# An attention and expert kernel: keys and queries of a head loaded in single transfers, the base of the experts' output formed on TensorE, and a planner that knows when the attention output is divided

## The chip, the cores and the metric

The kernel runs on one core of a Trainium2 chip. A core has five engines that run their own instruction streams and meet through semaphores: TensorE (PE in the profile), VectorE (DVE), ScalarE (ACT), GpSimd (POOL) and SyncE (SP), which here does nothing but issue DMAs. The metric is the device time of one execution in microseconds (us); the number for a kernel is the median of its runs. A profile is one further execution, with the hardware profiler on; its span goes from its first to its last instruction.

## The reference, cut to what matters

Two batches (B = 2) of N = 2048 tokens with D = 256 features go through one transformer layer. `mod` is six vectors per batch, made from `c`.

```python
h = layernorm(x) * (1 + ca) + sa
q, k, v = h @ Wq, h @ Wk, h @ Wv                 # 16 heads of 16
R = |i - j|;  R_hat = (1 + exp(v_h)) / (1 + exp(v_h - w_h * R))
scores = relu(q k^T) * R_hat ; causal ; softmax(scores / sqrt(16))
x = x + ga * (ctx @ Wo + bo)
h2 = layernorm(x) * (1 + cb) + sb                # xf: all 4096 tokens
s = softmax(h2 @ gate_w.T)                       # 8 experts
for each expert: take the 512 tokens with the largest s   (top_k)
    y = layernorm(h2[idx]) * ln_w + ln_b
    o = gelu(y @ fc1.T + b1) @ fc2.T + b2 ;  o *= s[idx]
    xf[idx] += o                                 # xf starts as h2
x = x + gb * xf
```

The last line means that a token's output is `x + gb*h2` plus `gb` times what experts add to it. The kernel writes `x + gb*h2` to the output first (this is what the experts' output is added to, here called the base), and then adds the experts' rows with an indirect accumulating DMA.

## The kernel before, in words

**Attention.** The work is cut into units (batch, head, query tiles): for a head, query tiles of 128 are packed as [0-3], [4,5], [6,7], and then 8 to 15 one by one, 11 units a head and 352 in all. A unit's steps are: scores `sc` on PE (L907; keys `kr` times queries `qr`, with 16 rows of contraction), DVE multiplies relu(sc) by the table `tb` (L920) and takes the maximum off (L927), POOL masks the diagonal (L932), PE transposes (L971), ACT takes the exponential (L979), PE multiplies with values `vg` (L1012). When a head is complete, DVE divides by the row sums into `ctx` (L1079, function `divide`).

PE keeps four row groups of 32 rows, so that the 16 rows of a head's keys are needed four times, at partitions 0, 32, 64 and 96. Keys and queries of all heads are first written to DRAM (`k_d`, `q_d`: tiles of 128 x 512, one for 8 heads and 512 tokens) and read back for each head. Before, each read is 16 rows of 512 numbers (32 KB): `keys` issues one for each of four chunks and four row groups, 16 a head; `queries` issues four for each group of four query tiles, 16 a head.

The order of issue on SP for a head h: around the head's first scores the next head's inputs are asked by `head_inputs` (the table `tb`, 1 MB, and the keys; values every fourth head), and the scores of query tile 4c ask for the query group two ahead. There are three buffers for query groups, and two each for keys and tables. SP works its list in order; an issue that has to wait for its buffer holds up all behind it.

**Planner.** The order of PE, DVE, ACT and POOL is written out by a planner in the program (`manual_schedule`): it keeps a clock for each engine (`plan.pe`, `plan.dve`, ...), and at each point chooses the next step of the attention or a "filler": a piece of a prologue (layernorm, q, k, v of the next 512 tokens) or of an epilogue (what follows attention for a group g of 512 tokens). The pieces of an epilogue name the pieces that they wait for; `made` has the planned time of each finished piece. The names used below: `turn` (PE transposes ctx, `trc`, L660, ACT copies it to cT), `project` (PE multiplies by Wo), `add` (adds x1), `stats`/`apply` (layernorm), `rows` (ACT writes z, the tokens as the experts want them, and a DMA of 128 KB takes them to `z_d`; two buffers), `gated` (h2 times gb) and `base` (adds x1, DMA to the output). `over()` is true when the last unit's scores have been issued. `late(i)` says whether fillers lag behind their pace. The last two heads (from unit PAIR_AT) are interleaved by query group.

**Search, listing, experts.** After attention the scores of all tokens lie in 128 x 256 numbers `rows`. A search over the bits of a float finds each expert's threshold, two bits a step in 15 steps: three DVE comparisons with a count (`ge`, L1511), one PE matmul that sums the counts over partitions (`pcnt`, L1516), and a few small DVE operations that set the next candidates. Between the matmul and its use, one piece of the remaining DVE list (`left["dve"]`, the last layernorm statistics) is put in, and ACT writes z rows that are ready. Then come `tot` and `p_off` (L1556, L1558), the listing of chosen tokens, and the gathers by POOL (`zt<-z_d`, L1656). Experts e = 0 to 7 each gather 4 x 128 rows, transpose (`trf`, L1671), do the two layers (`ph`, `pof`) and scatter-add.

For the last batch 16 `gated` and 16 `base` pieces are still undone when attention ends. `rest_of_output` issues them on POOL, each 128 x 256 (L625, the line of the helper `sum_or_product`), after the gathers of expert 0, each base with its DMA to the output:

```python
        gathered(0, s)
        rest_of_output()
```

Of the kernel before, what the change touches and what calls it, by code (L numbers as in the profile page):

```python
# [9 lines left out]
FP = mybir.dt.float32  # L10
# [4 lines left out]
ALU = mybir.AluOpType  # L15
# [4 lines left out]
P = 128  # L20
B = 2
N = 2048
# [150 lines left out]
def adaln_block_kernel(  # L173
# [30 lines left out]


    q_d = [[dram.tile([P, 512], FP, name=f"q_d_{b}_{i}") for i in range(HG * 4)] for b in range(B)]
    k_d = [[dram.tile([P, 512], FP, name=f"k_d_{b}_{i}") for i in range(HG * 4)] for b in range(B)]
    v_d = [[dram.tile([512, 8 * VW], FP, name=f"v_d_{b}_{i}") for i in range(HG * 4)] for b in range(B)]


# [41 lines left out]
    def turned(shape: list, name: str):  # L252

        return ps_tr.tile(shape, FP, name=name, tag=f"tr{plan.bank()}")
# [191 lines left out]
    def prologue(b: int, c: int, hT, first: bool):  # L446
# [56 lines left out]
        def qk(g: int, w_sb, dst, tag: str, parts: list):  # L503
            n = len(parts) * P
            pp = turned([P, n], f"p{tag}_{u}_{g}_{parts[0]}")
            for k in range(DC):
                nc.tensor.matmul(
                    pp, lhsT=w_sb[:, k, ts(g, P)], rhs=s["hT"][:, k, ds(parts[0] * P, n)],
                    start=(k == 0), stop=(k == DC - 1),
                )  # L510
            if parts[0] == 0:
                s[tag, g] = ev_p.tile([P, 512], FP, name=f"{tag}_{u}_{g}", tag="qk")
            nc.scalar.copy(s[tag, g][:, ds(parts[0] * P, n)], pp)
            if parts[-1] == 3:
                nc.sync.dma_start(out=dst[b][g * 4 + c], in_=s[tag, g])
            return plan.small(427 * len(parts), 120 + 120 * len(parts), 0)

        def val(g: int, parts: list):
# [42 lines left out]
        return work  # L561


    def keys(b: int, h: int, c: int):
        for r in range(RG):
            nc.sync.dma_start(
                out=inputs[b, h][0][ds(32 * r, HD), ts(c, 512)],
                in_=k_d[b][h // 8 * 4 + c][ts(h % 8, HD), :],
            )

    def values(b: int, h: int, c: int):
        nc.sync.dma_start(
# [3 lines left out]
            ),  # L576
        )

    def head_inputs(b: int, h: int, chunks=range(4)):
        kr = krp.tile([P, N], FP, name=f"kr_{b}_{h}", tag="kr")  # L580

        tb = tabp.tile([P, N], FP, name=f"tb_{b}_{h}", tag="tab")
        row = rhat_d[h, :]
        nc.sync.dma_start(
            out=tb, in_=bass.AP(tensor=row.tensor, offset=row.offset, ap=[[1, P], [1, N]])
        )

        if h % 4 == 0:
            vg = vgp.tile([P, NQ * 4 * VW + HD], FP, name=f"vg_{b}_{h}", tag="vg")
            nc.gpsimd.memset(vg[:, NQ * 4 * VW :], 0.0)  # L590
        else:
            vg = inputs[b, h - 1][2]
        inputs[b, h] = (kr, tb, vg)
        for c in chunks:
            keys(b, h, c)
            if h % 4 == 0:
                values(b, h, c)

    def queries(at: int):

        if at >= len(asked):
            return
        b, h, c = asked[at]
        qr = qrp.tile([P, 512], FP, name=f"qr_{b}_{h}_{c}", tag="qr")
        for r in range(RG):
            nc.sync.dma_start(
                out=qr[ds(32 * r, HD), :], in_=q_d[b][h // 8 * 4 + c][ts(h % 8, HD), :]
            )
        qrs[b, h, c] = qr


    def epilogue(b: int, g: int):
# [52 lines left out]

        def project(k: int):
            po = turned([P, D], f"po_{u}_{k}")
            for f in range(HG):
                nc.tensor.matmul(
                    po, lhsT=s["cT", k][:, f, :], rhs=wo_sb[:, b, f, :],  # L670
                    start=(f == 0), stop=(f == HG - 1),
                )
            if over():
                x1 = s["x1"][:, k, :]
                nc.vector.tensor_tensor(x1, po, x1, ALU.add)
                s["added", k] = True
                return plan.small(853, 0, 350)

            nc.scalar.copy(s["h2"][:, k, :], po)
            return plan.small(853, 380, 0)  # L680

        def add_to(k: int):
            if ("added", k) in s:
                return 0.0
            x1 = s["x1"][:, k, :]
            return sum_or_product(x1, s["h2"][:, k, :], x1, ALU.add)

# [33 lines left out]
            skip("widen", k)  # L721
            return plan.small(0, 0, 430)

        def skip(name: str, k: int):
            work[:] = [p for p in work if p[3] != (first, name, k)]
            made[first, name, k] = 0.0

        def root():
            s["root"] = root_of(*s["vr", 3], f"3_{u}")
# [18 lines left out]
        def move(k: int):  # L748
            h2 = s["h2"][:, k, :]
            if ("centered", k) in s:  # L750
                nc.vector.scalar_tensor_tensor(
                    h2, h2, s["rs2"][:, k : k + 1], sb, ALU.mult, ALU.add
                )
                return plan.small(0, 0, 430)
            return sum_or_product(h2, h2, sb, ALU.add)


        def gated(k: int):
# [59 lines left out]
            work[0][4].extend((first - 4, x, k) for x in ("base", "gate") for k in K)  # L818
        for k in K:
            piece("pe", 218, turn, "turn", k, ("project", k - 2) if k > 1 else ("begin", 0))  # L820
            if g == 3 and k < 2:
                work[-1][4].append((first - 2, "gate", k + 2))
            piece("pe", 853, project, "project", k, "turn", "bias")
# [58 lines left out]
    FIRST_OUT = 11  # L882
    SOON = ("load", "bias", "begin", "turn", "project", "add")
    LOW = ("gated", "base", "rows", "stats3", "power3", "root3", "shift3")
    row_free = [0.0, 0.0]
    OPEN = 4
    groups_out = [[epilogue(b, g) for g in range(4)] for b in range(B)]
# [3 lines left out]
    def over():  # L891
        return begun[0] == len(units)
# [165 lines left out]
    def divide():  # L1058

        b, h, gs = dividing.pop(0)  # L1060
        if gs[-1] == 3:
            undivided.remove((b, h))
        if h == 0:
            ctxs[b] = cxp.tile([P, NQ, D], FP, name=f"ctx_{b}", tag="ctx")
        cs = sums[b, h][0]
        rc = avp.tile([P, NQ], FP, name=f"rc_{b}_{h}_{gs[0]}", tag="rc")
        g0, gn = gs[0], len(gs)
        nc.vector.reciprocal(
            rc[:, 0 : 4 * gn].rearrange("p (q o) -> p q o", o=1),
            cs[:, ds(4 * g0, 4 * gn), HD:VW],  # L1070
        )

        o = ctxs[b][:, ds(4 * g0, 4 * gn), ts(h, HD)].rearrange("p (g j) f -> p g j f", j=4)
        if h % 2:
            o = bass.AP(
                tensor=o.tensor, offset=o.offset + 3 * D,
                ap=[list(o.ap[0]), list(o.ap[1]), [-D, 4], list(o.ap[3])],
            )
        nc.vector.tensor_tensor(  # L1079
            o, cs[:, ds(4 * g0, 4 * gn), 0:HD].rearrange("p (g j) f -> p g j f", j=4),  # L1080
            rc[:, 0 : 4 * gn].rearrange("p (g j o) -> p g j o", j=4, o=1)
            .broadcast_to([P, gn, 4, HD]),
            ALU.mult,
        )
        plan.small(0, 0, 200 + 150 * gn)
        if h == H - 1:
            add(groups_out[b][gs[0]][1], False)
            i = turns[-1]["i"] if turns else 0
            more(max(i, H * len(PACKS)), FIRST_OUT * len(PACKS) if b < B - 1 else 12)
# [40 lines left out]

    def make(w: dict, at: int):
        p = w["work"].pop(at)
        w["past"] = p[2]() or 0.0
        if not w["in_order"]:
            made[p[3]] = w["past"]
        if not w["work"]:
            fillers.remove(w)
# [143 lines left out]

    def late(i: int):

        return ahead_by(i) < (1.5 if plan.now == "f" else -1.5)

    def ahead_by(i: int) -> float:

# [9 lines left out]
    with tc.manual_schedule(engines={ENG.PE, ENG.DVE, ENG.Activation, ENG.Pool}):  # L1297
# [10 lines left out]
            arrived(c)  # L1308

        def arrived(c: int):  # L1310
            keys(0, 0, c)
            queries(c)
            values(0, 0, c)
            there[c] = plan.act + 5000
            if c == 3:
                head_inputs(0, 1)
                after_chunks()
# [76 lines left out]
    def weights(e: int):  # L1394
# [14 lines left out]
            lambda p=p: (p[2](), done.add(p[3])) for p in pending if p[0] == "dve"  # L1409
        ],  # L1410
        "act": [p for p in pending if p[0] == "act"],
        "pool": [p for p in pending if p[0] == "pool"],
    }

    def ready_rows():

# [3 lines left out]
                done.add(p[3])  # L1420
                left["act"].remove(p)

    def rest_of_output():
        for p in left["pool"]:
            assert all(x in done for x in p[4])
            p[2]()
            done.add(p[3])

    with tc.manual_schedule(engines={ENG.PE, ENG.DVE, ENG.Activation, ENG.Pool}):
        b1_sb = rt.tile([P, E * FC], FP, name="b1_sb")  # L1430
# [12 lines left out]
        nc.gpsimd.iota(steps, pattern=[[0, TOP // 2 + 1], [1, 3]], base=1, channel_multiplier=0)  # L1443
        nc.gpsimd.iota(twice, pattern=[[2, TOP // 2 + 1], [0, 3]], base=0, channel_multiplier=0)
        nc.vector.tensor_tensor(steps, steps, twice, ALU.logical_shift_left)
        thr = rt.tile([P, 1], I32, name="thr0", tag="thr", bufs=2)
        nc.vector.memset(thr, 0)

# [58 lines left out]
        for bit in range(TOP, -1, -2):  # L1507
# [9 lines left out]
            if bit:  # L1517
# [2 lines left out]
                    base, steps[:, bit // 2 - 1, :], thr.broadcast_to([P, 3]), ALU.bitwise_or  # L1520
                )

            if left["dve"]:
                left["dve"].pop(0)()
                ready_rows()
# [14 lines left out]

        while left["dve"]:
            left["dve"].pop(0)()
            ready_rows()

        hit = rt.tile([P, 2, 2, P], FP, name="hit")
        for k, op in ((0, ALU.is_gt), (1, ALU.is_equal)):
# [173 lines left out]
    with tc.manual_schedule(engines={ENG.PE, ENG.DVE, ENG.Activation, ENG.Pool}):  # L1722
# [5 lines left out]
            one_hot(0, s, i)  # L1728
            listed(0, s, i)
        gathered(0, s)  # L1730
        rest_of_output()

        warm = ps_h.tile([P, CAP], FP, name="warm_up", tag="h")
        for k in range(WARM):
# [72 lines left out]
```

## Time and profile before

| | us |
|---|---|
| runs of the kernel before | 1744.17, 1748.26, 1731.19 (median 1744.17) |
| profiled execution, its own time | 1757.64 |
| its span | 1755.9 |
| mean granted PE clock | 0.928 |
| PE busy, PE weight loads busy | 1626.8, 1137.9 |
| DVE, ACT, POOL busy | 1320.8, 839.7, 410.3 |
| moved by DMA | 135.31 MB, 77 GB/s on average |

A head takes about 38 to 40 us while the clock is full. The first scores are at 33.3 us, attention ends at about 1415, the search lasts from about 1437 to 1475, and the experts from 1500 to the end.

How to read it: in a group of instructions, "line engine operation out<-in shapes xcount | busy us, mean ns | idle before, releaser" says how long the engine stood idle ahead of that group, and which engine's instruction or DMA ended the wait. In a table of windows each engine has its busy time in that stretch and, in brackets, its instructions; the last three columns are the clock granted to PE (1.00 is full), the busy share of the 16 DMA engines, and GB/s. Lines with "SPq" are DMA issues: their duration is what SP took to issue, and "us to landing" what the data took to arrive. In a list of waits the numbers are: us in total, times, the longest.

### The profile page before, as it was taken

What the parts mean: (1) busy time and instruction counts of PE and PEld (TensorE: products, weight loads), DVE (VectorE), ACT (ScalarE), POOL (GpSimd) and SP (SyncE); (2) the same over time, 40 slices, a digit from 0 to 9 for tenths busy, and PEclk for the clock granted to TensorE, in tenths of its full rate; (3) what the DMA queues carried; (4) which work ended last, traced back from release to release, by engine and by line L of the source; (5) the groups of instructions that cost most, each with busy time, mean ns of one, the idle gap of its engine ahead of it and who ended that gap; (6) DMA issues with size and microseconds to landing.
All of it is one profiled execution on the core that took longest, in us unless ns stands there. A gap on an engine that the chain in (4) does not pass through costs nothing. (4 is left out here: it accounts for less than half of the span.)

```text
span 1755.9 us, 58026 instructions
## 1 busy us (share of the span) xinstructions
PE 1626.8 (93%) x24205; PEld 1137.9 (65%) x24205; DVE 1320.8 (75%) x2533; ACT 839.7 (48%) x2348; POOL 410.3 (23%) x814
## 2 busy tenths in 40 slices
PE   8999999999999999999999999899999952899997
PEld 6767766677766677666666666566666642567674
DVE  5477798888878787688989998689876868554532
ACT  2455665565655556456655565456544520121211
POOL 1111121211111113122232331223311210833332
PEclk9899999999999899699999999799988965899999
DMA  6332232233222222121231322223110030344431
GB/s 225 97 102 81 69 87 69 71 88 98 68 75 70 71 77 82 50 63 51 69 84 50 92 77 66 67 66 97 53 56 5 9 123 24 100 112 115 110 92 22
DMA packets 111286, 135.31 MB, mean 77 GB/s; under 512 B 43313, under 2 KB 81841, under 8 KB 106929
## 3 DMA queue, kind: packets, MB, share of 16 engines
q1 hardware_dynamic: 104880, 123.08, 23.3%
q0 software_dynamic: 6144, 8.52, 2.8%
q8 instruction: 191, 3.13, 0.7%
q14 instruction: 71, 0.57, 0.1%
HBM read 105.82 MB, written 25.70 MB: 75 GB/s over the span
## 5 line engine op out<-in xcount | busy, mean ns | idle before, releaser
L979 ACT ACTIVATE pt<-tr 128x512 f32<-128x512 f32 (+7 forms) x1628 | 632.4, 458 | 516.5 <-PE tr L971 513.5
L920 DVE CUSTOM_DVE_ANT_0 s<-sc,tb 128x128 f32<-128x128 f32 (+15 forms) x512 | 647.5, 1288 | 237.7 <-PE sc L907 218.4
L971 PEld LDWEIGHTS tr<-ident,s 64*128 64x128 f32 x8704 | 349.8, 144 | 240.2 <-issue 97.7
L971 PE MATMUL tr<-ident,s 64*128 64x64 f32 x8704 | 446.4, 237 | 11.0 <-ACT pt L979 6.0
L932 POOL TENSOR_SCALAR_AFFINE_SELECT s<-s 128x128 f32<-128x128 f32 x512 | 171.2, 348 | 1073.0 <-DVE s L927 627.1
L927 DVE TENSOR_SCALAR s<-s,m 128x128 f32<-128x128 f32 (+15 forms) x512 | 392.0, 791 | 9.1
L907 PE MATMUL sc<-kr,qr 16*128 16x384 f32 (+15 forms) x4096 | 370.5, 453 | 25.1 <-DVE m L920 14.2
L1012 PE MATMUL avb<-pt,vg 128*32 128x128 f32 x8704 | 368.9, 289 | 3.7 <-ACT pt L979 2.9
L1012 PEld LDWEIGHTS avb<-pt,vg 128*32 128x32 f32 x8704 | 236.7, 114 | 68.3 <-issue 23.4
L907 PEld LDWEIGHTS sc<-kr,qr 16*128 16x128 f32 x4096 | 165.2, 192 | 84.8 <-DVE m L920 46.0
L1686 ACT ACTIVATE hT<-ph,b_sb 128x512 f32<-128x512 f32 x64 | 43.9, 687 | 183.3 <-PE ph L1682 183.3
L1682 PE MATMUL ph<-yT,w 128*128 128x512 f32 x256 | 116.7, 600 | 0.9 <-DVE yT L1672 0.5
L1706 PE MATMUL pof<-w,hT 128*128 128x256 f32 x512 | 115.0, 383 | 0.0
L1706 PEld LDWEIGHTS pof<-w,hT 128*128 128x128 f32 x512 | 97.3, 192 | 13.3 <-issue 0.5
L1711 DVE TENSOR_TENSOR o<-pof,b2b 128x256 f32<-128x256 f32 x32 | 13.6, 424 | 89.8 <-PE pof L1706 89.8
L1682 PEld LDWEIGHTS ph<-yT,w 128*128 128x128 f32 x256 | 46.8, 190 | 49.2 <-issue 46.2
L1713 POOL DMA_INDIRECT out_dram<-o,idx x32 | 51.1, 1597 | 95.5 <-DVE o L1712 22.9
L625 POOL TENSOR_TENSOR h<-h,modr 128x256 f32<-128x256 f32 x68 | 51.3, 767 | 0.0
L1656 POOL DMA_INDIRECT zt<-z_d,idx x32 | 33.5, 1047 | 66.9 <-issue 49.2
L261 POOL TENSOR_TENSOR rr<-rv,mhalf 128x4 f32<-128x4 f32 x24 | 24.6, 1028 | 92.0 <-DVE rv L260 91.9
L1028 ACT COPY avs<-avb 128x128 f32<-128x128 f32 x128 | 36.2, 283 | 18.0 <-PE avb L1012 16.9
L1046 PE MATMUL trs<-ident,avs 128*128 128x128 f32 x128 | 42.9, 335 | 1.9 <-ACT avs L1028 0.7
(185 smaller groups left out, 1155.7 us busy)
## 6 DMA issues: line engine op xcount, KB each, us to landing
tb<-rhat_d SPq DMA_DIRECT2D x32, 1024.0 KB, 6.2
kr<-k_d SPq DMA_DIRECT2D x512, 32.0 KB, 1.9
qr<-q_d SPq DMA_DIRECT2D x512, 32.0 KB, 1.8
w<-in_fc1T_dram SPq DMA_DIRECT2D x8, 1024.0 KB, 4.8
w<-in_fc2T_dram SPq DMA_DIRECT2D x8, 1024.0 KB, 5.5
v_d<-vt SPq DMA_DIRECT2D x16, 272.0 KB, 2.4
vg<-v_d SPq DMA_DIRECT2D x32, 136.0 KB, 3.0
xt<-in_x_dram SPq DMA_DIRECT2D x8, 512.0 KB, 4.3
```

The lines of the kernel that those rows point to most:

```text
L625: nc.gpsimd.tensor_tensor(out, a, c, op)
L907: nc.tensor.matmul(sc[:, r, ds(at, w)], lhsT=qr[ds(32 * r, HD), ts(q % 4, P)], rhs=kr[ds(32 * r, HD), ts(r, w)], start=True, stop=True,)
L920: nc.vector.tensor_tensor_reduce(out=s[:, ds(RG * at, n)].rearrange("p (r w) -> p r w", w=w), in0=sc[:, :, ds(at, w)], in1=rev, scale=1.0, ...
L927: nc.vector.tensor_scalar(s[:, ds(RG * at, n)], s[:, ds(RG * at, n)], 0.0, m[:, j : j + 1], ALU.max, ALU.subtract,)
L932: nc.gpsimd.affine_select(out=diag, in_=diag, pattern=[[-1, P]], compare_op=ALU.is_ge, fill=MASKED, base=0, channel_multiplier=1,)
L971: nc.tensor.transpose(trs[a][:, at + k, :], u["s"][ts(a, TR), ts(k0 + k, P)], ident[ts(a, TR), ts(a, TR)],)
L979: nc.scalar.activation(u["pt"][:, ds(k0, n), ts(a, TR)], trs[a][:, ds(at, n), :], AF.Exp)
L1012: nc.tensor.matmul(avb[ds(32 * j, 32), grp["slot"], :], lhsT=inputs[b, h][2][:, ds((4 * kt + h % 4) * VW, 32)], rhs=u["pt"][:, k, :], star ...
L1682: nc.tensor.matmul(ph, lhsT=s["w"][0][:, k, ts(f, P)], rhs=s["yT"][:, k, :], start=(k == 0), stop=(k == DC - 1),)
L1686: nc.scalar.activation(s["hT"][:, f, :], ph, AF.Gelu_apprx_tanh, bias=b1_sb[:, e * FC + f : e * FC + f + 1])
L1706: nc.tensor.matmul(po, lhsT=s["hT"][:, f, ts(i, P)], rhs=s["w"][1][:, f, :], start=(f == 0), stop=(f == FC - 1),)
L1713: nc.gpsimd.indirect_dma_start(out=outr, out_offset=bass.IndirectOffsetOnAxis(ap=s["idx"][:, i : i + 1], axis=0), in_=o, in_offset=None, b ...
```

## The change

1. **Keys and queries in single transfers.** `k_d` becomes two tiles of 128 x 2048 a batch, one for each 8 heads. `to_groups` fills all four row groups with one DMA: its source is 32 rows (the 16 wanted and the 16 after them), read four times over by a leading dimension with step 0. Keys of a head come in one DMA of 1 MB, queries of a group in one of 256 KB. For the last head of each eight, where no 16 rows follow, it issues four transfers of 16 rows. The first head's keys still come chunk by chunk.
2. **x1 is added on PE at the tail.** Once `over()` holds, `project` adds x1 with one more matmul (the identity times x1) into the same bank, and ACT copies the sum to x1; the DVE addition and the piece `add` go.
3. **The base on TensorE.** The 32 POOL operations go. In each step of the search, between the matmul `pcnt` and its use, `base_made` and `base_turned` are called: one transposes a tile of h2 (two 128 x 128 transposes, an ACT copy `bT`), the other, one step later, multiplies it by the diagonal of gb and adds x1 with the identity (four 128 x 128 fp32 matmuls), copies to x1 on ACT and starts the output DMA. `gates_apart` makes the two diagonals on DVE ahead of the search. What the 15 steps leave is done in the loop after them.
4. **The planner.** The turn of a group waits in the plan for `context`, the planned time of its division. `make` moves an engine's planned clock on to the time at which the piece's inputs are there. `late(i)` is true from PAIR_AT on.

The diff, without the changed signatures and the assertions:

```diff
-    k_d = [[dram.tile([P, 512], FP, name=f"k_d_{b}_{i}") for i in range(HG * 4)] for b in range(B)]
+    k_d = [[dram.tile([P, N], FP, name=f"k_d_{b}_{i}") for i in range(HG)] for b in range(B)]
...
-                nc.sync.dma_start(out=dst[b][g * 4 + c], in_=s[tag, g])
+                to = k_d[b][g][:, ts(c, 512)] if dst is k_d else q_d[b][g * 4 + c]
+                nc.sync.dma_start(out=to, in_=s[tag, g])
...
-    def keys(b: int, h: int, c: int):
-        for r in range(RG):
-            nc.sync.dma_start(
-                out=inputs[b, h][0][ds(32 * r, HD), ts(c, 512)],
-                in_=k_d[b][h // 8 * 4 + c][ts(h % 8, HD), :],
-            )
+    def to_groups(dst: bass.AP, src: bass.AP, h: int):
+
+        if h % 8 == 7:
+            for r in range(RG):
+                nc.sync.dma_start(out=dst[ds(32 * r, HD), :], in_=src[ts(7, HD), :])
+            return
+        at = src[ds(h % 8 * HD, 32), :]
+        nc.sync.dma_start(
+            out=dst, in_=bass.AP(tensor=at.tensor, offset=at.offset, ap=[[0, RG]] + [list(x) for x in at.ap])
+        )
+
+    def keys(b: int, h: int, cs: list):
+        n = 512 * len(cs)
+        to_groups(
+            inputs[b, h][0][:, ds(512 * cs[0], n)], k_d[b][h // 8][:, ds(512 * cs[0], n)], h
+        )
...
     def queries(at: int):
...
-        for r in range(RG):
-            nc.sync.dma_start(
-                out=qr[ds(32 * r, HD), :], in_=q_d[b][h // 8 * 4 + c][ts(h % 8, HD), :]
-            )
+        to_groups(qr, q_d[b][h // 8 * 4 + c], h)
...
         def project(k: int):
             po = turned([P, D], f"po_{u}_{k}")
+            x1 = s["x1"][:, k, :]
+            adds = over()
             for f in range(HG):
                 nc.tensor.matmul(
                     po, lhsT=s["cT", k][:, f, :], rhs=wo_sb[:, b, f, :],
-                    start=(f == 0), stop=(f == HG - 1),
+                    start=(f == 0), stop=(f == HG - 1 and not adds),
                 )
-            if over():
-                x1 = s["x1"][:, k, :]
-                nc.vector.tensor_tensor(x1, po, x1, ALU.add)
-                s["added", k] = True
-                return plan.small(853, 0, 350)
+            if adds:
+                nc.tensor.matmul(po, lhsT=ident, rhs=x1, start=False, stop=True)
+            if adds:
+                nc.scalar.copy(x1, po)
+                there = plan.small(853 + 427, 400, 0)
+                skip("add", k, there)
+                return there
...
             piece("pe", 218, turn, "turn", k, ("project", k - 2) if k > 1 else ("begin", 0))
+            work[-1][4].append(("context", b, g))
...
         if h == H - 1:
+            made["context", b, gs[0]] = plan.dve + 150
+            for g in gs[1:]:
+                made["context", b, g] = plan.dve + 150
             add(groups_out[b][gs[0]][1], False)
...
         p = w["work"].pop(at)
+        if not w["in_order"]:
+
+            kind = "dve" if over() and p[0] == "pool" and p[3][1] not in LOW else p[0]
+            if kind in ("dve", "act", "pool"):
+                setattr(plan, kind, max([engine(kind)] + [made[x] for x in p[4]]))
...
-        return ahead_by(i) < (1.5 if plan.now == "f" else -1.5)
+        return i >= PAIR_AT or ahead_by(i) < (1.5 if plan.now == "f" else -1.5)
...
-    def rest_of_output():
-        for p in left["pool"]:
-            assert all(x in done for x in p[4])
-            p[2]()
-            done.add(p[3])
+    diag = rt.tile([P, DC, P], FP, name="diag")
+    half_made = []
+
+    def gates_apart():
+        for f in range(DC):
+            nc.vector.tensor_tensor(diag[:, f, :], ident, modr[:, 1, 3, ts(f, P)], ALU.mult)
+
+    def base_turned():
+        if not bases:
+            return
+        first, _, k = bases.pop(0)
+        tr = ps_t.tile([P, DC, P], FP, name=f"trb_{first}_{k}", tag="t")
+        for f in range(DC):
+            nc.tensor.transpose(tr[:, f, :], tiles[first]["h2"][:, k, ts(f, P)], ident)
+        bT = rt.tile([P, DC, P], FP, name=f"bT_{first}_{k}", tag="bT", bufs=2)
+        nc.scalar.copy(bT, tr)
+        half_made.append((first, k, bT))
+
+    def base_made():
+        if not half_made:
+            return
+        first, k, bT = half_made.pop(0)
+        x1 = tiles[first]["x1"][:, k, :]
+        pb = ps_o.tile([P, D], FP, name=f"pb_{first}_{k}", tag="o")
+        for f in range(DC):
+            nc.tensor.matmul(pb[:, ts(f, P)], lhsT=bT[:, f, :], rhs=diag[:, f, :], start=True, stop=False)
+            nc.tensor.matmul(pb[:, ts(f, P)], lhsT=ident, rhs=x1[:, ts(f, P)], start=False, stop=True)
+        nc.scalar.copy(x1, pb)
+        nc.sync.dma_start(
+            out=outr[ds((first // 4) * N + (4 * (first % 4) + k) * P, P), :], in_=x1
+        )
...
         nc.vector.tensor_tensor(steps, steps, twice, ALU.logical_shift_left)
+        gates_apart()
...
+            base_made()
+            base_turned()
             if left["dve"]:
                 left["dve"].pop(0)()
                 ready_rows()
...
-        while left["dve"]:
-            left["dve"].pop(0)()
+        while left["dve"] or bases or half_made:
+            if left["dve"]:
+                left["dve"].pop(0)()
             ready_rows()
+            base_made()
+            base_turned()
...
         gathered(0, s)
-        rest_of_output()
```

## The prediction

> **What bounds the kernel now.** I read the page's head and slices, then the waits of PE, then windows around each wait, then the DMA queue. The page's first lines:
>
> ```profile
> span 1755.9 us, 58026 instructions
> PE 1626.8 (93%) x24205; PEld 1137.9 (65%) x24205; DVE 1320.8 (75%) x2533; ACT 839.7 (48%) x2348; POOL 410.3 (23%) x814
> PE   8999999999999999999999999899999952899997
> PEclk9899999999999899699999999799988965899999
> ```
>
> PE is the bound; only slices 33 and 34 (the search) leave it idle. But 93% busy is not 93% at speed: the clock row dips twice in the attention (0.6 and 0.7). The waits of PE from 700 to 1440 us, and windows beside two of them:
>
> ```profile
> PE tr L971 <- ACT pt L979: 6.0, 3, 4.6
> PE trc L660 <- DVE ctx L1079: 5.4, 2, 2.8
> 680.00:700.00 20.00, 19.82 (x419) 14.17 (x418) 18.57 (x34) 11.63 (x33) 11.30 (x23) 1.00 0.32 95
> 720.00:740.00 20.00, 20.00 (x259) 13.71 (x261) 12.10 (x26) 8.51 (x22) 2.70 (x8) 0.50 0.27 82
> 1100.00:1120.00 20.00, 15.32 (x173) 9.14 (x172) 10.50 (x14) 6.73 (x19) 4.53 (x9) 0.66 0.19 58
> ```
>
> A 2.8 us wait at 712 is followed by 34 us at clock 0.5 (granted clock, 714 to 748), where PE, fully busy, issues 259 matmuls in 20 us instead of 419: about 38% of such time is lost. **So a wait of PE costs itself and a multiple of itself.** Any wait that the change removes or makes must be priced so.
>
> The wait of 4.6 us at 1102 ends on ACT; ACT itself waited for a DMA (first line, ACT's waits), and SP's timeline says why that DMA was late:
>
> ```profile
> ACT z L788 <- DMA z_d<-z: 5.0, 1, 5.0
> 1094.70 10.02 SPq L566 DMA_DIRECT2D kr<-k_d  x16
> 1104.82 0.84 SPq L792 DMA_DIRECT2D z_d<-z  x2
> ```
>
> Sixteen key loads take SP 10 us to issue, and a write of z, whose buffer ACT needs, stands behind them. At 1300.2 queries stand behind 16 key loads in the same way: a 1.45 us wait of PE, then clock 0.61 over 1300 to 1320.
>
> **Part 1, keys and queries in single transfers.** SP issues 512 key and 512 query loads of 32 KB; now it is 47 and 176. Ten microseconds of issue per head go. Bytes double, since 32 rows are read for each group and 16 are used: 1 MB per head for keys, 256 KB per query group. What one such transfer takes is the central unknown. The nearest row by size:
>
> ```profile
> tb<-rhat_d SPq DMA_DIRECT2D x32, 1024.0 KB, 6.2
> kr<-k_d SPq DMA_DIRECT2D x512, 32.0 KB, 1.9
> qr<-q_d SPq DMA_DIRECT2D x512, 32.0 KB, 1.8
> ```
>
> By this row keys land in 6.2 us. But tb is read with a slowest dimension of 128; the new transfer is read as [4 repeats][32 rows][2048]. The Trainium skill, "DMA: Bandwidth & Descriptors", section "Why a DMA increments its semaphore by 16 and not by 1", says that a DMA is spread over the largest number up to 16 that divides the slowest dimension of both patterns: here 4, against 16 for every load that before's trace shows. By the rule, 32 packets of 8 KB fall to each of four engines. Packets of 8 KB took 309 to 347 ns in the trace (504 where the queue was fullest): 32 × 0.31 to 0.35 = 10 to 11 us, and about 1.8 us fixed (the landing of a 32 KB load): 12 to 13 us. Queries: 32 packets of 2 KB at 84 ns = 2.7, + 1.8 = 4.5 us. No row here speaks against the rule, so I take four engines, and keep 6.2 us as the other end.
>
> Does PE feel it? Keys are asked a head (about 39 us) ahead, so 13 us is hidden. The last query group of a head isn't: counted from the start of a head's scores, SP issues group 2 at −2.5, the next head's keys behind it, the next table at about 0, group 3 at 1.2 us. Per engine that is 64 + 256 + 64 + 64 = 448 KB, 18 to 20 us at the rates above: group 3 lands at 17 to 18.5. Its first scores came at 21 to 27 in the heads I timed (median 24). Covered by 3 us at the tightest: cost 0. Without that cover see the second rival.
>
> *Start.* The first head still loads by chunk, on four engines: the first queries land at some 36.3 instead of 33.3, +3. Behind them the second head's 1 MB of keys (issued about 73.5) holds four engines until about 87; query group 3 of head 0 lands at 93.5 instead of the 81.4 at which it is wanted: with the cold clock +9. Together +12 (16 engines: −2).
>
> *z writes.* The wait at 1102 (4.6 us and 20 us at 0.66, about 10 us) goes, but two later z writes stand behind 1 MB of keys on four engines: I place them 5 us (head 24) and 3 us (head 27) late for ACT, with the cold clock 17 us. Net +7 (16 engines: −10).
>
> *Queries at 1300.* With two issues instead of 36, on time: 1.45 us and the cold 20 us go, −8.
>
> *Code loading.* PE's idle time put to "issue" (518, 601, 1258 us, 1.2 to 1.9 us each) lies near the ends of table loads. With four engines held longer I add one more with its cold clock, +4 (ends 0 and +12).
>
> **Part 2, the planner's dependency on the division.** Both trc waits (712 and 1334) are turns placed before ctx (L1079, 527 ns at the head's end) was written. They are worth 5.4 us and (34 + 7) × 0.38 = 16, together 21. The turns now wait in the plan for the division. PE's order is unchanged up to the first batch's epilogue (about 700 us) and reshuffled after. What stands in for the turn is PE work that exists anyway, but a planner that holds pieces back pays some of it later. I take −15, ends −21 and +5.
>
> **Part 3, the sum under the experts' output moves from POOL to the search.** POOL's rows from 1490 to 1532, and PE's waits from 1440 to 1560:
>
> ```profile
> L625 POOL TENSOR_TENSOR x<-h,x 128x256 f32<-128x256 f32 x16 | 13.9, 872 | 1.3
> L625 POOL TENSOR_TENSOR h<-h,modr 128x256 f32<-128x256 f32 x16 | 13.9, 870 | 0.0
> PE pcnt L1516 <- DVE ge L1511: 25.6, 13, 2.0
> PE trf L1671 <- DMA zt<-z_d,idx: 6.6, 4, 5.0
> ```
>
> The 32 operations hold POOL from 1496.8 to 1525.3. Expert 1's indices are ready at 1518.9, its four gathers start at 1525.5, and trf waits 5.0 us to 1531.1. Without POOL's 27.8 us the gathers start at 1519 and land before pof of expert 0 ends (1526.1): **−5**. Next late is then pof itself, PE's own work.
>
> In the search each of 15 steps lasts 2.555 us, PE waits 1.97 of it. Added per step: two transposes and four fp32 128x128 matmuls, two ACT copies, one output DMA. Nearest rows: transposes trg, trc 0.27 to 0.48; pv, two fp32 matmuls, 0.71 hot and 1.22 cold: 2.4 + 0.6 = 3.0 us at clock 0.5, 1.85 at 1. Hot, it fits in the 1.97; cold, each step grows by 1.0. The search ran at 0.50 because PE idled; filled, it should warm after some steps. Five cold steps would be 5, ten 10; most should be warm, so I take +2, and 2 for the late tot/p_off turn at its end and the two products for the diagonal (0.15 each, DVE): **+4**, ends 0 and +17. ACT is nearly idle there (2.2 of 20 us), and its copies feed nothing in the chain of the search. The 16 output DMAs move with it to a stretch at 26 to 53 GB/s: 0.
>
> *Adding x1 on PE in project:* some 11 matmuls of 128x256 (0.3 to 0.5 us) more, as many DVE additions (0.42) fewer, at the tail of the last batch where DVE and PE alternate: 0, ends ±4.
>
> **The sum** on the profiled execution, 1757.6 (span 1755.9 and 1.7 around it): +12 + 7 − 8 + 4 − 15 − 5 + 4 + 0 = −1. That execution was 0.8% over the median of the runs (1744.2); the difference is carried to the median: **1743 us**. One per cent, 17 us, is about what a measurement of this kernel can tell from no change.
>
> **Rivals.**
> 1. *The width costs nothing* (16 engines, or four without harm): start −2, z −10, queries −8, code 0, the rest as above: −2 − 10 − 8 − 15 − 5 + 4 = −36, **1708**. For it: the 6.2 us of tb, and SP as the visible culprit twice. Against it: the rule.
> 2. *Queries become late in many heads, slower.* Place: PE before the first scores of query group 3, behind 448 KB per engine. Point: from −2.5 to 21 less 1.8 fixed are 21.7 us, so below 20.6 KB/us (8 KB packets over 400 ns) the early heads stall; at 504 ns group 3 lands near 28, later than every head's need. Price: 2 us of wait and some 18 us at clock 0.5 (7) = 9 per stalled head. With six of 30 heads: −1 + 54 = +53, **1797**; with all, 2000 and more. For it: 504 ns was seen, and the margin is 3 us. Against: it was seen with 16 engines moving 374 GB/s; four move about 100.
> 3. *The plan's gain doesn't come*: the reshuffled order of fillers makes other waits, 0 or +5 in place of −15: **1758 to 1763**.
>
> **How the numbers follow.** Forecast 0.38 (faster 0.08, within 1% 0.22, slower 0.08, by the ends of start, z and search); rival 1 0.26 (0.23, 0.03, 0); rival 2 0.24 (0, 0.02, 0.22); rival 3 0.12 (0.02, 0.03, 0.07). Together 0.33, 0.30, 0.37. The range reaches to rival 1 and to rival 2 with six heads, 1700 to 1797; outside are the worse half of rival 2 and the best of rival 1. The likeliest case's own range is 1723 to 1765.
>
> **What would show it.** Keys: landing of the 1 MB transfers 12 to 13 us (four engines) or 6 (sixteen), and a row of PE waiting for qr. Start: query group 3 of head 0 awaited near 82 us. Plan: no trc wait for ctx, no slice at 0.6 near 720. Search: step length 2.6 to 3.6 us and its granted clock over 0.5. Experts: trf's 5 us gone. I am wrong if queries are awaited once per head, or if the clock dips stay while their causes go.

## The result, and the profile after

The changed kernel takes 1794.5 us (median of four runs, 1790.1 to 1797.3) against 1746.2 us for the kernel before (four runs on the same chip): 1.0288 of before, 95% interval 1.022 to 1.0357. The profiled execution took 1794.5 us with a span of 1792.8, 36.9 us more than the span before. The profiled execution of the kernel before (1757.6 us) is one of its slower ones, so the two traces differ by less than the 48 us between the medians. Forecast was 1743; 1794.5 lies at the upper end of the range, close to the 1797 that rival 2 gave.

The head of the page after, the same lines as before:

```profile
span 1792.8 us, 57537 instructions
PE 1641.3 (92%) x24377; PEld 1157.0 (65%) x24377; DVE 1308.3 (73%) x2528; ACT 855.0 (48%) x2391; POOL 382.5 (21%) x780
PE   7869999899999999999999999698989977799997
PEclk8869999999999999999899999867899976899998
```

PE has new holes in slices 1 to 3 and a deeper one at slice 26; the clock is down in slice 3 (0.6) and in slices 26 to 29 (0.6 to 0.8). The slice that holds most of the search (34) is fuller, 0.7 in place of 0.2, but its clock is still 0.6. The longest waits of PE after (total, times, longest in us):

```profile
PE sc L921 <- DMA qr<-q_d: 44.0, 9, 19.0
PE tr L985 <- ACT pt L993: 24.8, 13, 13.3
PE pb L1473 <- ACT bT L1463: 7.2, 14, 2.0
```

Before, these were 4.5 us for qr and 6.0 us for tr; the wait for bT is new, and belongs to part 3. The waits for ctx (trc) are gone.

**Where the time went.** I took the first scores of each head from both traces and subtracted. After minus before: +5.4 us at head 0; +23.8 at head 1; another +6.8 in head 5; 0.6 or less in most heads between; −4.6 and −2.9 in heads 11 and 13 (waits put to issue, at 518 and 601 us before, that are gone there); −7.5 and −4.6 in heads 15 and 16, where before had the ctx wait at 712 and the cold stretch behind it; +2.8, +4.7 and +2.5 in heads 17, 19 and 20; +3.8, +10.1, +13.1 and +6.5 in heads 25 to 28. After head 28 the sum is +55.8. The last two heads (30 and 31) and what follows up to the search, the second ctx wait and late queries of before among them, give 20 back: the first `pcnt` stands at +37.4. The search is 6.8 us longer, the experts 7.3 shorter.

**The start.** SP's timeline after, with what SP issued (start, duration):

```profile
75.62 0.34 SPq L516 DMA_DIRECT2D k_d<-k  x1
78.07 1.11 SPq L572 DMA_DIRECT2D kr<-k_d  x2
80.81 0.34 SPq L516 DMA_DIRECT2D q_d<-q  x1
82.64 0.38 SPq L536 DMA_DIRECT2D v_d<-vt  x1
100.14 1.15 SPq L572 DMA_DIRECT2D qr<-q_d  x2
```

and SP's longest wait from 27 to 110 us:

```profile
SPq L572 <- DMA q_d<-q: 17.1, 1, 17.1
```

The second kr at 78 is the 1 MB of keys for head 1. The write of the queries (q_d, issued at 80.8) stands behind it in the queue; SP does not issue the load of these queries before the write has landed, 19 us after its own issue; PE waits 19.0 us, to 106.7. The records of single packets show the width: the 128 packets of 8 KB of these keys run from 83.5 to 99.0 us, and their durations add up to 3.7 packets at a time (443 ns each on average, median 372). Tables (tb), with as many packets of this size, ran mostly 9 to 13 at a time in the kernel before and were through in 4 to 6 us. **Four engines, as the slowest dimension of 4 says** (the Trainium skill, "DMA: Bandwidth & Descriptors", section "Why a DMA increments its semaphore by 16 and not by 1"), and 15.5 us in place of the 10 to 11 of packets in my sum. The first of these packets moves 4.9 us after SP issues the transfer, not 1.8.

**The writes of z.** ACT's waits after, from 1100 to 1250 us:

```profile
ACT z L800 <- DMA z_d<-z: 23.4, 2, 15.1
```

SP's timeline ahead of the longer one:

```profile
1110.04 0.52 SPq L572 DMA_DIRECT2D qr<-q_d  x1
1110.61 0.51 SPq L572 DMA_DIRECT2D kr<-k_d  x1
1112.57 1.86 SPq L804 DMA_DIRECT2D z_d<-z  x2
1114.53 1.19 SPq L595 DMA_DIRECT2D tb<-rhat_d  x1
1115.81 0.54 SPq L572 DMA_DIRECT2D qr<-q_d  x1
1118.10 6.40 SPq L777 DMA_DIRECT2D out_dram<-x  x1
```

and the window in which it lies (PE's busy time and matmuls first, then the other engines; the granted clock third from the end):

```profile
1120.00:1140.00 20.00, 6.72 (x118) 4.60 (x110) 4.50 (x8) 4.03 (x10) 2.35 (x6) 0.66 0.36 106
```

SP issues the keys at once now, as predicted; z is issued 2 us after them. But it stands behind the queries and keys in the same queue: ACT waits 15 us for its buffer, PE 13, and does 118 matmuls in 20 us. Even the issue of an output DMA takes SP 6.4 us here, where the other 128 KB output DMAs of this stage take 0.3 to 0.4.

### The profile page after: what moved, and what is told of

Same layout as the page of the kernel before. It is cut to its first block, busy times and chain, and to the rows that moved or that the text cites. A ratio compares the mean times of both kernels' runs of the same rounds, so it can differ in the third digit from the quotient of the medians.

```text
span 1792.8 us, 57537 instructions
## 1 busy us (share of the span) xinstructions
PE 1641.3 (92%) x24377; PEld 1157.0 (65%) x24377; DVE 1308.3 (73%) x2528; ACT 855.0 (48%) x2391; POOL 382.5 (21%) x780
## 5 line engine op out<-in xcount | busy, mean ns | idle before, releaser
L921 PE MATMUL sc<-kr,qr 16*128 16x384 f32 (+15 forms) x4096 | 364.1, 452 | 63.2 <-DMA qr<-q_d 44.0
L507 PE MATMUL pk<-hT,wk_sb 128*128 128x128 f32 (+1 forms) x232 | 42.0, 322 | 1.2 <-ACT hT L495 0.9
```

What stands on the lines that cost most here:

```text
L921: nc.tensor.matmul(sc[:, r, ds(at, w)], lhsT=qr[ds(32 * r, HD), ts(q % 4, P)], rhs=kr[ds(32 * r, HD), ts(r, w)], start=True, stop=True,)
```

## The experiments

Ratios are to runs of the kernel before on the same chip, with 95% intervals; the change itself is 1.0288. First: is it the transfers, their width, their bytes, or the planner?

**All loads in 16-row transfers** (`e1_rows16`), four for a head's keys:

```diff
-        if h % 8 == 7:
-            for r in range(RG):
-                nc.sync.dma_start(out=dst[ds(32 * r, HD), :], in_=src[ts(7, HD), :])
-            return
-        at = src[ds(h % 8 * HD, 32), :]
-        nc.sync.dma_start(out=dst, in_=bass.AP(..., ap=[[0, RG]] + ...))
+        for r in range(RG):
+            nc.sync.dma_start(out=dst[ds(32 * r, HD), :], in_=src[ts(h % 8, HD), :])
```

> The changed kernel, but every key and query load is made as its eighth heads are: four transfers of 16 rows, 128 KB for keys and 32 KB for queries, no unused rows. Theory A (one transfer is carried by four DMA engines, and what stands behind it on SP's queue waits): the start is back within 3 us of before, the waits for qr at heads 5, 13, 19 and 29 and the two ACT waits for z_d are gone; about 1735 (1725 to 1750). Theory B (the doubled bytes do it): the same time as A here, so this run alone doesn't part them. Theory C (the planner's new order makes the waits, not the transfers): stays over 1780.

Measured 1739.8 us, 1.0023 (0.9995 to 1.0052). No ACT wait of 2 us or more for z_d is left, and the waits for qr of over 1 us are at the start (5.3 and 3.4 us). Theory C falls. But 1735 was the middle of what was expected, and the time is that of before, though the planner's gain should be in it.

**Four transfers of 32 rows** (`e2_rows32`): the bytes of the change, sixteen engines.

```diff
+        n = HD if h % 8 == 7 else 32
+        for r in range(RG):
+            nc.sync.dma_start(out=dst[ds(32 * r, n), :], in_=src[ds(h % 8 * HD, n), :])
```

> The changed kernel, but its single transfer is cut into four of 32 rows each: the same bytes as the change, twice what is needed, with a slowest dimension of 32 on both sides. Theory A (four engines): as fast as the run with 16 rows to within 6 us, keys landing in some 6 us in place of 16. Theory B (bytes): stays near 1790. Theory C: over 1780.

Measured 1737.9 us, 1.0002 (0.9961 to 1.0044): as fast as with half the bytes. So the doubled bytes cost nothing that shows; the width does.

**Part 1 undone** (`e3_old_keys`: `keys`, `queries`, `head_inputs` and `k_d` as before, the rest as changed):

> The changed kernel with part 1 undone: keys and queries per chunk, 16 issues of 32 KB, as before; planner, addition on PE and search as changed. Theory A: what is left of the change gains the two waits for ctx (12 us seen at heads 15 and 16) and some 7 us for experts, and loses 7 us in the search: about 1732 (1722 to 1745). Theory C: 1780 or more.

Measured 1721.1 us, 0.9894 (0.9858 to 0.993): the rest of the change gains 1.1%, and part 1 costs 3.9% of the time before (1.0288 against 0.9894).

**Part 1 alone on the kernel before** (`e4_keys_only`):

> The kernel before with part 1 alone. Theory A: start +24, a few heads with late queries +15, z writes late in the second batch +20 to +35, queries at 1300 no longer late -8: about 1800 (1780 to 1820). Theory C: within 1% of before.

Measured 1841.1 us, 1.0503 (1.0385 to 1.0621), above what I expected. In the old plan's order z writes meet the keys at four places, with ACT waits of 10.8, 4.2, 15.1 and 6.9 us, instead of two; and the ctx waits stay. The same loads cost 5.0% in one order of fillers and 3.9% in another.

**Eight engines** (`f1_eight`): one transfer, one dimension turned, for all heads.

```diff
-        at = src[ds(h % 8 * HD, 32), :]
+        at = src[ts(h % 8, HD), :]
         nc.sync.dma_start(
-            ... ap=[[0, RG]] + [list(x) for x in at.ap]
+            ... ap=[[0, 2 * RG]] + [list(x) for x in at.ap]
```

> The changed kernel with one dimension of the key and query loads turned: one transfer still, 16 rows read eight times over ([8 repeats][16 rows]) in place of 32 rows read four times; as many bytes, for all heads. Theory A (the slowest dimension sets the number of DMA engines): eight engines, keys in some 8 us in place of 16; most of the start's 24 us and of the late queries and z writes go: 1750 (1738 to 1768), that is within 2% above before. Theory B (one large transfer, or its bytes, cost as such, however many engines): 1780 or more.

Measured 1848.6 us, 1.0584 (1.0533 to 1.0634), worse than the change: a miss, and an instructive one. Its width is as Theory A says: the 128 packets of the second head's keys take 9.0 us, 7.5 at a time. The start's wait falls from 19.0 to 10.8 us, and no query is late after it. Two z waits of 8.3 and 8.7 us remain. But something else has come; PE's waits in this kernel:

```profile
PE avb L1022 <- issue: 27.8, 9, 5.7
PE tr L981 <- issue: 21.0, 8, 4.7
PE sc L917 <- DMA qr<-q_d: 19.3, 4, 10.8
PE sc L917 <- issue: 11.7, 4, 3.8
```

"Issue" is a wait for nothing that the profile names: 61 us in 22 waits up to 1400 us, against 4.3 in 5 for the change. One of them, in PE's timeline:

```profile
476.48 0.46 PE L981 MATMUL tr<-ident,s 64*128 64x64 f32 x8
480.71 0.59 PE L981 MATMUL tr<-ident,s 64*128 64x64 f32 x6 [3.77 <-issue]
```

The packets of the instruction queue are 16 KB each, and there are 191 to 193 of them in every kernel here; the 24205 matmuls and as many weight loads of the kernel before are 189 times 256, so most bring PE's instructions (256 to 16 KB, as the Trainium skill has it, "Runtime: NRT & Kernel Launch", section "Instruction fetch mechanics"). Such a packet runs from 477.6 to 479.0, and PE goes on at 480.7. The first of the 22 waits lies at 21 us; in each of the other 21 (0.6 to 5.7 us) one such packet ends 1.2 to 1.7 us before PE resumes, with 38 to 63 packets of 8 KB moving beside it or in the microsecond before. So the reading is that PE waited for its own program. The packets themselves are not slow (1.0 to 1.6 us in these waits, median 1.2 in this kernel), so that the delay lies before they start. The page calls such a crossing "mostly hidden"; here it isn't. Another page, "DMA: Bandwidth & Descriptors", section "Queues, rings and completion order", says that an engine changes between rings only after a whole packet, of up to 64 descriptors. By an estimate from that section, 16 rows of 8 KB, which is one engine's share here, held together would take some 9 us at the 577 ns that is the median here, so a wait of 2 to 6 us for a turn fits; no run here shows how rows are held together. That the eight engines hold the one that carries PE's instructions, and the four do not, would explain why the change itself shows hardly any such wait; no run here names the engine.

**z on another queue** (`f4_z_act`): `nc.scalar.dma_start` for the writes of z.

> The changed kernel with one edit: the writes of z are issued by ACT, and so go to another DMA queue than keys and queries. Theory A1 (the write waits its turn in the queue behind the keys): the ACT waits of 15 and 8 us for z_d go, and the cold stretches with them: -25 (-15 to -35), 1770. Theory A2 (the four engines themselves are taken, whichever queue): the waits stay at 5 us and more, within 10 of the change.

Measured 1797.4 us, 1.0321 (1.0271 to 1.0371): no gain. In the profile the ACT waits have shrunk:

```profile
ACT z L800 <- DMA z_d<-z: 11.1, 3, 6.3
```

With them heads 25 to 28 take 174 us in place of the change's 193 (159.9 before): that is what the z writes cost there, as far as one profile each can tell. But from head 29 to the listing of tokens 13 us are lost again, 8.5 of them in the search: its clock stays at 0.5 from 1470 to 1528 us, while it rose twice in the change's. The profiled execution took 1783.2 us, the other three, of which no trace was kept, 1795 to 1805. Half a hit for each theory: the queue sets part of the wait; that the rest is due to the four engines which z still shares with the keys is likely, not shown.

**Keys or queries?** `h2_keys_single` loads the queries as before and keeps the single keys; `h3_queries_single` the reverse.

> The changed kernel with the queries loaded by four transfers of 16 rows again; keys stay single. Queries then go over all engines, but stand in the same queue behind the keys' four. Theory A: most of the cost stays, 1785 (1770 to 1795), with the start's wait for the third query group over 12 us. Rival: the late queries come from their own four-engine transfers, and the time falls to 1740 or less.

> The changed kernel with the keys loaded by 16 transfers of 32 KB again; queries stay single. Theory A: a query group takes 4 engines for some 3 us, nothing long stands in front: within 8 us of the kernel with both kept old (0.989 of before). Rival: 1770 or more.

Measured 1.0023 (0.9985 to 1.0061) for the single keys, 0.9946 (0.9901 to 0.9991) for the single queries. The first was a miss: against 0.9894 with neither, keys alone cost 1.3% and queries alone 0.5% (hardly more than the intervals), but both together 3.9%. In h2 the start's wait is there in full (19.8 us, head 1 is 20.4 us behind the kernel with neither), but after it no query is late, and one z wait of 5.2 us is left in the attention:

```profile
PE sc L924 <- DMA qr<-q_d: 26.3, 3, 19.8
PE tr L988 <- ACT pt L996: 8.7, 13, 3.6
```

In h3 the start has a shorter wait of the same kind (PE's waits from 70 to 110 us), and head 1 is 9.7 us behind; later no z wait of 2 us is left:

```profile
PE sc L921 <- DMA qr<-q_d: 10.1, 1, 10.1
```

So the start is two thirds the keys' doing and one third the queries', and there the costs add: 20.4 and 9.7 alone, 29.3 together. These are about the whole of the 1.3% and 0.5% (some 22 and 9 us). What doesn't add comes later: the two long z waits and the four late query groups of the change are there only when keys and queries load the same four engines, with 256 KB each for keys and another 256 KB each for queries in every head.

**The start alone** (`h4_start`): loads of the first batch's heads 0 (keys, queries) and 1 (keys) in 16-row transfers, the rest as changed.

> The changed kernel, with the loads of the first batch's first two heads alone (keys of heads 0 and 1, queries of head 0) as transfers of 16 rows. Theory A: the start's 24 us fall to 6 or less, everything later stays: -18, about 1776 by the scale of the first comparison, ratio to before 1.017 (1.012 to 1.024). Rival: the start's waits are made by the order of SP's list, not by the width of the transfers, and stay.

Measured 1.0197 (1.0108 to 1.0286), 0.9% or 16 us below the change: as expected, though the two intervals overlap. In the profiles head 1 comes 26.6 us sooner than in the change: the wait for query group 3 of head 0 is 3.0 us in place of 19.0. The z waits remain (12.8 and 10.1 us).

**Parts 3 and 4 by themselves, on the kernel before:**

> The kernel before with part 3 alone (the base made on TensorE in the search, no POOL work beside expert 0). By the traces of before and after the search lasts 7 us longer and the experts end 7 us sooner: 0 (-4 to +4). Rival: POOL's 28 us had held more than the four gathers, and the part is worth -8 or better; or the search loses 15 us where no fill warms the clock, +8.

> The kernel before with part 4 alone (context, planned clocks moved on, late() true from PAIR_AT). Theory: the two waits for ctx go with the cold stretch of 34 us behind the first: -16 (-10 to -22), which is all that the change without part 1 gained. Rival: the gain of the change without part 1 comes from the addition of x1 on PE at the tail, and this run gains under 6.

> The kernel before with one piece of part 4 alone: the turns wait in the plan for the division. Theory: the wait of 2.8 us at 712 us and the cold stretch behind it go: 0.990 (0.986 to 0.995), nearly all that part 4 gave. Rival: the planned clocks that make() moves on, or late(), give it, and this run is at 0.997 or above.

> The kernel before with another piece of part 4 alone: late() true from the last two heads on, so that fillers are put in without a pace there. Theory: it moves fillers out of the tail after the last scores into the last heads, 0 to -6 us: 0.996 to 1.000. Rival: 0.993 or less, that is half of what part 4 gave.

Part 3 alone: 0.9969 (0.9934 to 1.0004). Part 4 alone: 0.9896 (0.9859 to 0.9933). Of its pieces, `context` alone: 0.989 (0.9814 to 0.9966), with no trc wait for ctx left; `late` alone: 0.9997 (0.9962 to 1.0032). The whole gain of the change is those few lines that tell the planner when ctx is written. The kernel before with them is as fast as all of the change without part 1, and both beat both kernels. (Part 2 and the moved clocks of part 4 were not run alone.)

The gain lies only in part where the two waits were. `late` alone keeps both; this is the first of them (PE's waits from 700 to 740 us) and the window behind it:

```profile
PE trc L660 <- DVE ctx L1079: 2.8, 1, 2.8
720.00:740.00 20.00, 19.78 (x395) 14.38 (x391) 16.23 (x33) 11.29 (x31) 4.28 (x11) 0.99 0.33 98
```

The same wait, but 395 matmuls and a clock of 0.99 in the window for which the prediction shows 259 and 0.50. The clock is at 0.5 for 34 us around this wait in the profile of the kernel before, for 10 us here, for 7 in e4 and for 3 in f2. So the price of the wait changes from execution to execution, and the 34 us were a dear one. Against the profile of `late`, `context` is 17 us ahead when the search starts: 15 of them come from heads 30 and 31 and the stretch up to the search, where the second ctx wait lies (2.6 us, then 7 us at 0.5), 3 from heads 15 and 16, and elsewhere gains and losses nearly cancel. The z wait at 1102 is gone as well, which makes head 25 11 us shorter, though head 26 loses 6 again. What else the new order does in the last two heads was not taken apart.

**Why do sixteen engines not keep that 1%?** e1 and e2 carry part 4, yet are only level with before. Two trials: `h1_rows16_2k` cuts the four 128 KB transfers into pieces of 2 KB, and `i1_spread` asks the four over several units of the head.

```diff
-    k_d ... dram.tile([P, N], ...)
+    k_d ... dram.tile([4 * P, 512], ...)
...
+        src = k_d[b][h // 8].rearrange("(c p) f -> p c f", p=P)
+        ... in_=src[ts(h % 8, HD), cs[0] : cs[0] + len(cs), :]
```

> Parts 2 to 4 of the change, with a third form of loading: keys of a head in four transfers, one for each row group, of 16 rows by 4 chunks by 512 numbers, so 128 KB in pieces of 2 KB (k_d is kept by chunk); queries in four of 32 KB as before. Theory P (the 16-row run with 128 KB in pieces of 8 KB lost some 18 us against the old 16 issues because 8 KB packets on all engines delay PE's instruction fetch): waits of PE put to issue fall from 13.6 to about 6 us and the time is that of the old loads, 0.989 of before or better (to 0.985). Theory Q (four large transfers at once, however cut, are what delays it): 1.000 of before, waits for issue 12 us and more.

> As the run with 16 rows (four transfers of 128 KB for the keys of a head), but only the first of the four is asked at the head's second unit, the other three at its fourth, fifth and sixth. Theory Q (the burst holds the engine from which PE's instructions come): waits of PE for issue fall from 12 to 14 us to 7 or less and the time to 0.990 of before (0.985 to 0.995). Rival (the loss lies at the start, where the first two heads' loads share one tile and wait for its writes): issue may fall, the time stays at 0.997 to 1.003.

Measured 1.0008 (0.9969 to 1.0047) for pieces of 2 KB, with 13.2 us of waits for issue in the attention: packet size isn't it. Spread: 0.9947 (0.9899 to 0.9994), but 14.1 us of such waits, which was to fall to 7: perhaps half of the loss comes back (by the middle values; the intervals reach from none to all of it), not for the reason given. In one profile each, the four kernels with large key loads on sixteen engines have 12 to 14 us of waits for issue in 10 to 12 waits; with the old small loads it is 6.4 us in 6, and head 1 comes 6.4 us sooner than in e1 and 2.5 sooner than in h1. These two sizes and their cold stretches are of the order of the missing 18 us; which it is stays open.

## Why the prediction was wrong, point by point

The step that failed is the pricing of part 1. The sum gave its start, z writes, queries and code loading +15 us; measured it is 3.9%, some 69 us. The rest of the change was put at −16 and gained 1.1%, some 18.

- **The width of the transfer: right.** Four engines, by the rule against the tb row. The size was off: 15.5 us of packets, not 10 to 11, and the last packet 20.4 us after the issue, where 12 to 13 were forecast for the landing. A packet took 443 ns on average. The 309 to 347 ns were taken for the cost of a packet, but in the bursts of tables in the kernel before the averages were already 389 to 492 ns.
- **The start, the step that failed first.** +12 in the sum, 23.8 measured. I saw that keys stand before query group 3, and priced a late load. What I missed is the write of q_d: it stands behind the keys as well, and SP holds every later issue until it has landed (17.1 us). A store that a later load needs makes one queue wait for itself twice.
- **The z writes, the largest mis-sized term.** 5 and 3 us of ACT's waits in the sum, net +7 with the clock; measured 15.1 and 8.2 us, and 33.5 us in heads 25 to 28, of which 20 go when z has a queue of its own. I had placed the writes behind the keys alone; they stand behind queries too, 64 KB per engine each, and behind an SP that itself stalls on issue.
- **"Group 3 lands at 17 to 18.5, covered by 3 us at the tightest": failed in four heads** (5, 13, 19, 29: waits of 4.0, 2.1, 2.3 and 3.2 us). That is rival 2's mechanism, rarer than its six heads; together with start and z writes it gives rival 2's time, by another sum. That rival 2's number came out is luck.
- **Queries at 1300 (−8) and the z wait at 1102 (−10): credit for the wrong part.** They are gone, but the kernel with the old 16 loads and the new plan has no such wait either: its only z wait of 2 us or more is 3.1 us at 1407. `context` alone removes the z wait too, so it belonged to that order of fillers, not to SP's ten microseconds of issue alone. And the wait at 1300 ends in the trace on DVE (s, L927), 0.1 us after the queries landed: queries on time would have ended it no more than that sooner. So rival 1 (−36 with sixteen engines) was wrong in the same way: of four kernels with that width, three came out level with before and one 0.5% below.
- **Part 4: the number right, the reason in part luck.** −15 forecast, 1.04% or 18 us measured, and all of it from `context`. But the forecast priced 34 us of cold clock behind one wait of 2.8 us ("a wait of PE costs itself and a multiple of itself"), which one execution showed and others did not; and the measured gain lies mostly in the last two heads.
- **Part 3: right in sum.** Search +4 and experts −5 forecast; +6.8 and −7.3 in the change. The search hardly warmed up: most of its steps took 3.0 us at clock 0.5, the upper price of the two, as two windows in it show (granted clock third from the end):

```profile
1480.00:1500.00 20.00, 16.02 (x76) 15.18 (x76) 14.62 (x90) 6.62 (x17) 1.01 (x1) 0.59 0.21 72
1500.00:1520.00 20.00, 16.65 (x91) 15.41 (x90) 15.24 (x89) 7.10 (x20) 1.01 (x1) 0.67 0.21 74
```

  The wait of PE for zt is down from 6.6 us to this (waits from 1475 to 1560 us):

```profile
PE trf L1729 <- DMA zt<-z_d,idx: 2.0, 2, 1.0
```

- **Code loading (+4): not in the change** (4.3 us of waits up to 1400 us against 4.9), but with eight engines it is the largest wait (61 us).

## What to carry to other kernels

Before many small DMAs are merged, look at the slowest dimension of both patterns: a repeat with step 0 in front made the transfer narrow here, and its time that of its share on four engines (15.5 us of packets, where a table of the same size took 4 to 6). Then walk the queue behind it: what is written there, who needs that buffer, and which load waits for that write. A wait costs more than itself, but not by a fixed multiple: with the z wait of 13 us heads 25 and 26 took 25 us longer than with the old loads and the same plan, and a wait of 2.8 us was followed by 3 us of low clock or by 34. And split a bundle of edits before judging it: one of these, worth −1%, was hidden under another worth +4%. A cost that rests on one trace is better read from a second execution too.

## What the runs showed of the hardware that was not expected

- Narrow transfers seem able to starve PE of its own program: with eight engines taken by single transfers of 1 MB, PE stood 61 us in 22 waits of up to 5.7 us, with a 16 KB instruction packet in 21 of them; with four engines 4.3 us.
- The costs of two narrow loads on the same engines add at the start (20.4 and 9.7 us alone, 29.3 together), but not in the whole: 1.3% and 0.5% alone, 3.9% together.
- The same wait of PE, 2.8 us in the same order of instructions, came with 3, 7, 10 and 34 us of clock 0.5 in four executions.
- Twice the bytes on sixteen engines cost nothing that could be measured (1.0002 against 1.0023).
